# A layer norm plus masked attention kernel: the later groups' statistics taken from the transposed blocks again, the first two graphs interleaved by pieces, the second group's statistics made on ScalarE

## The chip, the cores and the metric

The kernel runs on one core of one Trainium2 chip. The time is the device time of one execution in microseconds. The kernel before has a median of 2884.72 us over three runs (2884.47 to 2885.43). Lower is better.

## The reference

128 graphs of 128 nodes with 768 features (`x`, float32), each with a 128 x 128 matrix of edge weights (`adj`). One layer is computed: a layer norm over the features without weights, a ReLU, three products with 768 x 768 weights, attention with 12 heads of 64 features that is masked and shifted by `adj`, and the sum with `x`.

```python
h = jnp.maximum(_layernorm(x, axis=-1), 0.0)
q, k, v = (split_heads(h @ W + b) for W, b in ((Wq, bq), (Wk, bk), (Wv, bv)))
scores = einsum('bhqd,bhkd->bhqk', q, k) / sqrt(64) + beta * adj[:, None]
scores = jnp.where(adj[:, None] > 0, scores, -9e15)
out = x + merge_heads(softmax(scores) @ v)
```

`_layernorm` is `(x - mean) / sqrt(var + 1e-5)`.

## The kernel before

The graphs are worked on in 32 groups of four (`GRP`); G counts the groups. A group goes through three slices of products on TensorE: `qk0` (queries and keys of heads 0 to 5), `v` (values) and `qk1` (queries and keys of heads 6 to 11). The normed, transposed activations of a group are taken as 2 x 3 blocks and each slice's weights as 3 x 3, and a slice is 15 products of sums of blocks (`PRODUCTS`, L66) in place of the 2 x 3 x 3 = 18 plain ones. A product is eight matrix multiplications (`product`, L355, all recorded at L371). The profile shows each as two passes, so a product is 16 passes. The products of a slice are added up in four PSUM banks, the chains a, b, c and d: when a product is done, its chain's bank is read by VectorE (L382, L387, L396) or ScalarE (L392), and only then may the chain's next product start. In the slice `qk0` of group 0 `plain_slice` (L520, products at L533) makes the 18 plain products.

The order of the work is written by hand: `todo[n]` holds what is issued after product n of a slice, and the loop over G (L647) fills it. The first part of group G's attention (`scores`, then three times `attend`) stands in its slices `v` and `qk1`, the second part in the slice `qk0` of group G+1. A scheduling layer then orders the instructions of each engine by when their inputs are expected, so that what has no gate moves ahead of its place. `tc.issue_after(i)` is such a gate: what is issued under it stays behind instruction i on its engine.

The lines that the change and the prediction touch:

- `load_x` (L151) loads a graph's x transposed by blocks of 32 x 32 (four loads of 96 KB), so that VectorE's 32 x 32 transposition (`to_hT`, L310, recorded at L315) makes the activations with features on the partitions. In this layout a row's features lie spread over four partitions. `stats` (L225) takes four statistics of 192 elements a graph; `moments_1` (L235, products at L241) and `moments_2` (L251, products at L255) add up the four partitions of a row with a small product with the matrix `mean8` each. Then follow the root on GpSimd (L262), the shift (L264) and the 16 norms on ScalarE (`norm`, L304, recorded at L308). Groups 1 and 2 go this way.
- Groups 3 to 31 instead take the statistics from a second copy of x in rows: `load_halves` (L271, two loads of 192 KB a graph), `row_stats` (L277, L283 and L284), `row_moments` (L286) with the root at L294, and 16 loads of 1 KB (L299) that spread the results over the partitions as `norm` wants them. `row_stats`, `norm` and `bias_1` of these groups are gated on the last addition of a product (`behind`, L653).
- `bias_1` (L332) and `bias_2` (L348) make the mask and shift of a group's scores out of `adj`; they use VectorE, a memset on GpSimd (L339) and a square on ScalarE (L346).
- Group 0's graphs 0 and 1 come in rows (L158). `rows_1` (L557) makes a graph's statistics and its root (L571), `rows_2` (L574) norms it in three pieces on VectorE (L579), transposes them on TensorE (L584) and applies the ReLU on ScalarE (L589). TensorE first runs 18 warm-up products (L595). Graph 0 is transposed as a whole and multiplied with the first column of weights, then `second` (L600) does the same for graph 1. Graphs 2 and 3 come in blocks.
- Group 1's x (L663) is loaded behind the weights of `qk1` (L674) on SyncE's queue; its statistics stand in slice `v` of G=0 (L695) on VectorE, beside the sums of weights (`sum_weights`, L197).

Of the kernel before, what the change touches and what calls it, by code (L numbers as in the profile page):

```python
# [10 lines left out]
F32 = mybir.dt.float32  # L11
# [6 lines left out]
P = 128  # L18
# [96 lines left out]
def direct(ctx, tc, x, adj, wq, bq, wk, bk, wv, bv, beta, out, bad):  # L115
# [115 lines left out]

    def halves(G, lo, hi, n):
        return st[G].rearrange("p b (h m) -> p b h m", h=2)[:, lo:hi, :, n]
# [34 lines left out]

    rows = {}

    def load_halves(G, g):  # L271

        for h in range(2):
            t = rows[G, g, h] = work.tile([P, VH], F32, tag=("adj", "adjT")[h], name=f"half_{G}_{g}_{h}", bufs=1)
            nc.sync.dma_start(t, x[G * GRP + g, :, h * VH:(h + 1) * VH])

    def row_stats(G, g):  # L277

        if g == 0:
            rows[G] = stat.tile([P, GRP, 2, nc.vector.BN_STATS_DIM], F32, tag="strow", name=f"strow_{G}", bufs=1)  # L280
            rows[G, "mv"] = stat.tile([P, GRP, nc.vector.BN_AGGR_DIM], F32, tag="mvrow", name=f"mvrow_{G}", bufs=1)
        for h in range(2):
            nc.vector.bn_stats(rows[G][:, g, h, :], rows[G, g, h])  # L283
        nc.vector.bn_aggr(rows[G, "mv"][:, g, :], rows[G][:, g])  # L284

    def row_moments(G):  # L286

        mv = rows[G, "mv"]
        ve = stat.tile([P, GRP], F32, tag="verow", name=f"verow_{G}", bufs=1)
        nc.vector.tensor_scalar(ve, mv[:, :, 1], EPS, None, op0=ALU.add)  # L290
        mean = stat.tile([P, GRP], F32, tag="meanrow", name=f"meanrow_{G}", bufs=1)
        nc.vector.tensor_scalar(mean, mv[:, :, 0], -1.0, None, op0=ALU.mult)
        t = stat.tile([P, 2, GRP], F32, tag="row2", name=f"row2_{G}", bufs=1)
        nc.gpsimd.tensor_tensor(t[:, 0], ve, nhalf.to_broadcast([P, GRP]), ALU.pow)  # L294
        nc.gpsimd.tensor_tensor(t[:, 1], mean, t[:, 0], ALU.mult)
        to = stat.tile([P, NB, 2, GRP], F32, tag="block2", name=f"block2_{G}", bufs=1)
        for b in range(NB):
            for a in range(NB):
                nc.sync.dma_start(to[a * SQ:(a + 1) * SQ, b], t[b * SQ:(b + 1) * SQ])  # L299
        for g in range(GRP):  # L300
            for b in range(NB):
                rstd[G, g * NB + b], shift[G, g * NB + b] = to[:, b, 0, g:g + 1], to[:, b, 1, g:g + 1]
# [217 lines left out]
    def plain_slice(G, sl, todo):  # L520

        n = 0
        for r in range(2):
            for j in range(3):
# [4 lines left out]
                for at, k in [(at, k) for at in parts for k in range(3)]:  # L529
                    a, b = A[G, f"A{r}{k}"], wt[sl, f"B{k}{j}"]  # L530
                    for i in range(2):
                        for c in range(2):
                            last = nc.tensor.matmul(p[:, i, at], b[:, c, i * P:(i + 1) * P], a[:, c, at],  # L533
                                                    start=(k == 0 and i == 0 and c == 0), stop=(c == 1),
                                                    skip_group_check=True)
                    if at is not parts[-1]:
                        if k == 2:
                            with tc.issue_after(last.ins):
                                second()
                        continue  # L540
                    if k == 2:
                        t = qk[G, sl, r, j] = work.tile([P, 2, H2], F32, tag="qk", name=f"{sl}_{G}_{r}_{j}", bufs=8)
                        oc = j + 3 * int(sl[2])
                        for i in range(2):
                            nc.scalar.activation(t[:, i, :], p[:, i, :], AF.Identity, bias=bqk[:, i, oc:oc + 1])
                        give(bank)
                    for f in todo.get(n, ()):
                        f()
# [329 lines left out]
```

## Time and profile before

| | us |
|---|---|
| median of three runs | 2884.72 |
| the profiled execution | 2884.47 |
| its span, from the first to the last instruction | 2882.7 |
| TensorE busy | 2872.4 |
| VectorE busy | 1955.9 |
| ScalarE busy | 806.5 |
| GpSimd busy | 316.9 |

The mean granted clock of TensorE is 0.999. A matrix multiplication of 128 x 256 is busy for 379 ns in the profile, but the passes overlap: one starts about every 0.108 us, so a product takes 1.727 us. A stage of TensorE (three slices, and the attention in between) takes 89.17 us.

The first stage, from the timeline:

| | start, us |
|---|---|
| warm-up products on TensorE | 2.15 |
| first graph's first statistics on VectorE | 4.79 |
| first piece of graph 0 (L579) | 8.24 |
| first transposition on TensorE (L584) | 8.90 |
| first plain product (L533) | 9.92 |
| graph 1's plain products | 13.46 |
| weights of `qk1`, first load issued | 27.70 |
| x of group 1, first load issued | 38.68 |
| slice `v` of G=0 | 43.10 |
| scores of G=0 (L417) | 73.35 |

How to read the profile's lines: a line of the timeline has the start and length in microseconds, the engine (PE is TensorE, PEld its weight loads, DVE VectorE, ACT ScalarE, POOL GpSimd, SP SyncE; a q behind the name means the engine's queue, which issues DMAs), the line of the kernel, the operation, the tile written and the tiles read, the shapes, the number of instructions merged, and in brackets how long the engine had been idle and what ended that. A line of the chain of waits has the start, the length and the group of instructions; the chain is followed back from the last instruction to what released each one.

### The profile page before, as it was taken

The page shows a single profiled execution, that of the slowest core. Times are in us where ns is not written, and L with a number is a line of the kernel's source. Part 1 is how long each engine was busy: PE and PEld are TensorE (multiplying, and loading weights), DVE is VectorE, ACT ScalarE, POOL GpSimd, SP SyncE. Part 2 cuts the span into 40 slices and gives each one's busy share as a digit, 9 for nine tenths or more (in the row PEclk, how much of TensorE's full clock was granted, in tenths as well). Part 3 has the DMA queues.
Part 4 walks back from the last instruction along what each step waited for, and adds up shares of the span by engine and source line. Part 5 has one row for each costly group of instructions (what it writes and reads, how often), then busy time and mean ns, then how long its engine had stood idle before and what let it go on. Part 6 is the DMA issues. An engine that isn't in the chain of part 4 may idle for free.

```text
span 2882.7 us, 81559 instructions
## 1 busy us (share of the span) xinstructions
PE 2872.4 (100%) x35330; PEld 2014.5 (70%) x35330; DVE 1955.9 (68%) x4511; ACT 806.5 (28%) x1750; POOL 316.9 (11%) x304
## 2 busy tenths in 40 slices
PE   9999999999999999999999999999999999999999
PEld 7666677666677676776667766677666677666776
DVE  7866666666666666666766666666666666666665
ACT  2422322232222323313232132322223222322221
POOL 1111111111011010110101101011101111110110
PEclk9999999999999999999999999999999999999999
DMA  6222233222232222322223322233222232222311
GB/s 167 77 62 76 58 84 87 73 71 67 75 88 80 64 74 68 87 86 63 76 65 86 90 60 82 60 85 88 69 75 62 80 88 75 69 70 72 88 41 39
DMA packets 413467, 218.31 MB, mean 76 GB/s; under 512 B 110384, under 2 KB 412720, under 8 KB 413104
## 3 DMA queue, kind: packets, MB, share of 16 engines
q1 hardware_dynamic: 411232, 212.66, 26.8%
q8 instruction: 277, 4.54, 0.6%
q10 hardware_dynamic: 1872, 0.40, 0.1%
q14 instruction: 86, 0.70, 0.1%
HBM read 162.14 MB, written 50.33 MB: 74 GB/s over the span
## 4 chain that ended last, share of the span: by engine, by line
PE 99%; DVE 1%; issue 0%; POOL 0%; POOLq 0%
PE bank L371 85%; PE bank L417 6%; PE bank L452 6%; PE bank L533 1%; PE bank L595 0%; DVE A L315 0%; DVE qk_T L206 0%; DVE qk L396 0%; DVE S L321 0%; DVE e L421 0%; PE bank L472 0%; PE bank L489 0%; PE bank L584 0%; DVE e L476 0%; DVE xo L497 0%
## 5 line engine op out<-in xcount | busy, mean ns | idle before, releaser
L371 PE MATMUL bank<-S,qk_T 128*64 128x256 f32 x7056 | 822.5, 379 | 0.8 <-ACT qk L392 0.8
L396 DVE TENSOR_TENSOR qk<-qk,bank 128x512 f32<-128x512 f32 x630 | 426.6, 677 | 411.8 <-PE bank L371 406.3
L371 PEld LDWEIGHTS bank<-S,qk_T 128*64 128x64 f32 x7056 | 503.8, 137 | 256.1 <-ACT e L424 5.2
L392 ACT ACTIVATE qk<-bank,bqk 128x256 f32<-128x256 f32 x756 | 315.8, 469 | 1149.3 <-PE bank L371 962.8
L457 POOL TENSOR_TENSOR xo<-xo,o 128x512 f32<-128x512 f32 x189 | 253.5, 1342 | 2075.2 <-DVE o L436 1777.9
L371 PE MATMUL bank<-S,qk_B 128*64 128x256 f32 x4032 | 478.2, 379 | 1.0 <-DVE qk L396 1.0
L371 PE MATMUL bank<-A,qk_T 128*64 128x256 f32 x4032 | 478.6, 379 | 0.4 <-DVE qk L396 0.4
L371 PE MATMUL bank<-v_T,S 128*64 128x256 f32 x3584 | 421.8, 380 | 0.0
L424 ACT ACTIVATE e<-e 128x512 f32<-128x512 f32 x378 | 227.8, 628 | 642.8 <-DVE e L421 641.8
L371 PEld LDWEIGHTS bank<-A,qk_T 128*64 128x64 f32 x4032 | 284.3, 137 | 137.0 <-DVE qk L396 0.5
L387 DVE TENSOR_TENSOR v<-v,bank 128x512 f32<-128x512 f32 x320 | 219.8, 687 | 232.6 <-PE bank L371 230.8
L371 PEld LDWEIGHTS bank<-S,qk_B 128*64 128x64 f32 x4032 | 278.6, 137 | 128.9 <-DVE qk L396 1.4
L371 PEld LDWEIGHTS bank<-v_T,S 128*64 128x64 f32 x3584 | 254.7, 137 | 130.4 <-issue 5.7
L421 DVE SCALAR_TENSOR_TENSOR e<-bank,biasT 128x512 f32<-128x512 f32 x378 | 231.7, 682 | 109.1 <-PE bank L417 109.1
L371 PE MATMUL bank<-v_B,S 128*64 128x256 f32 x2048 | 243.2, 379 | 0.0
L371 PE MATMUL bank<-v_T,A 128*64 128x256 f32 x2048 | 237.9, 379 | 0.0
L308 ACT ACTIVATE x<-x,block 128x192 f32<-128x192 f32 x464 | 217.3, 535 | 39.9 <-DMA block<-row 39.1
L452 PEld LDWEIGHTS bank<-v,e 128*64 128x64 f32 x6048 | 208.6, 138 | 27.3
L315 DVE STREAM_TRANSPOSE A<-x 128x256 f32<-128x256 f32 x378 | 211.8, 612 | 4.0 <-ACT x L308 4.0
L452 PE MATMUL bank<-v,e 128*64 128x65 f32 x6048 | 208.3, 221 | 0.0
L382 DVE TENSOR_TENSOR v<-bv_b,bank 128x512 f32<-128x512 f32 x192 | 131.8, 687 | 105.2 <-PE bank L371 105.2
L371 PEld LDWEIGHTS bank<-v_B,S 128*64 128x64 f32 x2048 | 147.1, 137 | 73.9
(90 smaller groups left out, 1603.6 us busy)
## 6 DMA issues: line engine op xcount, KB each, us to landing
x<-in_x_dram SPq DMA_DIRECT2D x504, 96.0 KB, 2.6
xo<-in_x_dram SPq DMA_DIRECT2D x189, 256.0 KB, 3.0
out_dram<-xo SPq DMA_DIRECT2D x189, 256.0 KB, 2.6
half<-in_x_dram SPq DMA_DIRECT2D x232, 192.0 KB, 2.8
adj<-in_adj_dram SPq DMA_DIRECT2D x128, 64.0 KB, 3.0
block<-row SPq DMA_DIRECT2D x464, 1.0 KB, 1.7
qk_T<-in_L_gnn_Wq_dram SPq DMA_DIRECT2D x10, 128.0 KB, 3.7
qk_T<-in_L_gnn_Wk_dram SPq DMA_DIRECT2D x10, 128.0 KB, 3.8
```

The costliest lines, as they stand in the source:

```text
L308: nc.scalar.activation(t, t, AF.Relu, bias=shift[G, n], scale=rstd[G, n])
L315: last = nc.vector.transpose(t[:, :, g * N:(g + 1) * N].rearrange("p c (b i) -> p c b i", i=SQ), src)
L371: nc.tensor.matmul(p[q:q + HD, i, :], lhs[:, q:q + HD], rhs, start=(first and i == 0 and c == 0), stop=(c == 1), skip_group_check=True)
L382: added[G] = nc.vector.tensor_tensor(o4, bias[:, None, :, :].to_broadcast([P, 2, 4, HD]), p.rearrange("p g (h d) -> p g h d", d=HD), ALU.a ...
L387: added[G] = nc.vector.tensor_tensor(o, o, got, ALU.add if sign > 0 else ALU.subtract)
L392: nc.scalar.activation(t[:, i, :], p[:, i, :], AF.Identity, bias=bqk[:, i, oc:oc + 1], scale=float(sign))
L396: added[G] = nc.vector.tensor_tensor(t, t, p, ALU.add if sign > 0 else ALU.subtract)
L417: nc.tensor.matmul(ps[oc, i][k:k + HD, g * N:(g + 1) * N], t[r, 1, at][:, k:k + HD], t[r, 0, at], start=True, stop=True)
L421: taken[0] = nc.vector.scalar_tensor_tensor(e, ps[oc, i].rearrange("p (g n) -> p g n", g=GRP), SCORE_CAP * ISCALE, biasT[G], op0=ALU.min, ...
L424: nc.scalar.activation(e, e, AF.Exp, scale=1.0 / ISCALE)
L452: nc.tensor.matmul(pa[q:q + HD, 2 * g + i, :], es[G, oc, i][:, 2 * r + g, q:q + HD], vt[G, "v", r, h // 4][:, 4 * g + h % 4, :], start=Tru ...
L457: nc.gpsimd.tensor_add(t, t, o.rearrange("p a (b j) d -> p (a b) (j d)", j=2))
```

## The change

1. `load_halves`, `row_stats` and `row_moments` go. Every group after the first has its statistics from the blocks (`stats`, `moments_1`, `moments_2`), and the gates `behind` go too. For groups 3 and later `stats` has no gate.
2. `stats_by_act` is new. It makes the statistics of group 1 on ScalarE: one pass with an accumulated sum for the mean of each block, one with an accumulated sum of squares for the deviations. It is called for graphs 0 and 1 at place 8 of `qk0` and for graphs 2 and 3 at place 0 of `v` of G=0. The norms of group 1 are placed one product sooner.
3. The loads of group 1's x for graphs 0 and 1 are issued ahead of the weights of `qk1` on SyncE's queue.
4. Graphs 0 and 1 of group 0 are interleaved: VectorE's operations stand in one line (`begin`), graph 1's statistics between graph 0's pieces, and TensorE's transpositions stand between the plain products (`PIECES`, `transposed`).

```diff
+    def stats_by_act(G, lo, hi):
+        if G not in st:
+            st[G] = stat.tile([P, GRP * NB, nc.vector.BN_STATS_DIM], F32, tag="st", name=f"st_{G}", bufs=2)
+        m = stat.tile([P, hi - lo], F32, tag=f"mean{lo}", name=f"mean_{G}_{lo}", bufs=1)
+        for step in range(2):
+            for n in range(lo, hi):
+                junk = work.tile([P, QD], F32, tag="e", name=f"junk_{G}_{step}_{n}", bufs=6)
+                t = xg[G, n // NB][:, n % NB, :]
+                if step:
+                    nc.scalar.activation(junk, t, AF.Square, bias=m[:, n - lo:n - lo + 1], scale=math.sqrt(0.5),
+                                         accum_out=st[G][:, n, 2:3])
+                else:
+                    nc.scalar.activation(junk, t, AF.Copy, scale=1.0 / QD, accum_out=st[G][:, n, 1:2])
+            if not step:
+                nc.scalar.activation(m, st[G][:, lo:hi, 1], AF.Copy, scale=-math.sqrt(0.5))
+        nc.scalar.copy(st[G][:, lo:hi, 4:6], st[G][:, lo:hi, 1:3])
...
-    def load_halves(G, g):
...
-    def row_stats(G, g):
...
-    def row_moments(G):
...
@@ plain_slice
-                for at, k in [(at, k) for at in parts for k in range(3)]:
...
-                    if at is not parts[-1]:
-                        if k == 2:
-                            with tc.issue_after(last.ins):
-                                second()
-                        continue
...
+                for g, at in enumerate(parts):
+                    for k in range(3):
+                        if len(parts) == 2:
+                            for piece in PIECES[g, k]:
+                                transposed(*piece)
+                        a, b = A[G, f"A{r}{k}"], wt[sl, f"B{k}{j}"]
                         for i in range(2):
+                            for c in range(2):
+                                line("pe", nc.tensor.matmul, p[:, i, at], b[:, c, i * P:(i + 1) * P], a[:, c, at],
+                                     start=(k == 0 and i == 0 and c == 0), stop=(c == 1), skip_group_check=True)
...
+    PIECES = {(0, 0): ((0, 0), (0, 1)), (0, 1): ((0, 2),), (0, 2): (), (1, 0): ((1, 0), (1, 1)), (1, 1): ((1, 2),),
+              (1, 2): ()}
...
+    def transposed(g, k):
+        bank = take()
+        p = bank[:, 0:H2].rearrange("p (c i) -> p c i", c=2)
+        for c in range(2):
+            line("pe", nc.tensor.transpose, p[:, c, :], rows[g, k][:, c, :], ident)
...
+        nc.scalar.activation(A[0, name][:, :, g * N:(g + 1) * N], p, AF.Relu)
+        give(bank)
...
+        stats_of(0, 0)
+        stats_of(0, 1)
+        root(0)
+        stats_of(1, 0)
+        piece(0, 0)
+        stats_of(1, 1)
+        piece(0, 1)
+        root(1)
+        piece(0, 2)
         for k in range(3):
+            piece(1, k)
...
@@ the loop over G
         if G + 1 < NG:
             for g in range(GRP):
-                then(6, lambda g=g: load_x(G + 1, g, (nc.sync,)))
+                if G:
+                    then(6, lambda g=g: load_x(G + 1, g, (nc.sync,)))
                 if G == 1:
                     then(11 + g, lambda g=g: behind_scores(stats, G + 1, g))
                 elif G:
-                    then((0, 5, 8, 11)[g], lambda g=g: load_halves(G + 1, g))
-                    then((4, 7, 10, 13)[g], lambda g=g: behind(row_stats, G + 1, g))
-            if G > 1:
-                raw = []
-                then(14, lambda: raw.append(load_adj(G + 1)))
-                then(14, lambda: row_moments(G + 1))
+                    then(11 + g, lambda g=g: stats(G + 1, g))
         if not G:
+            for g in range(2):
+                load_x(1, g, (nc.sync,))
             load_weights("qk1", AS_SUMMED)
+            for g in range(2, GRP):
+                then(6, lambda g=g: load_x(1, g, (nc.sync,)))
+            then(8, lambda: stats_by_act(1, 0, 2 * NB))
...
             at = 3 if G else 5
+            if not G:
+                then(0, lambda: stats_by_act(1, 2 * NB, 4 * NB))
             for g in range(GRP):
-                if not G:
-                    then(g, lambda g=g: stats(G + 1, g))
-                then(at + 5 + g, lambda g=g: behind(norm, G + 1, g) if G > 1 else norm(G + 1, g))
-            if G < 2:
-                then(at, lambda: got.extend(moments_1(G + 1, 0, GRP * NB)))
-                then(at + (3 if G else 2), lambda: moments_2(G + 1, 0, GRP * NB, *got[:2]))
+                then(at + (5 if G else 4) + g, lambda g=g: norm(G + 1, g))
+            then(at, lambda: got.extend(moments_1(G + 1, 0, GRP * NB)))
+            then(at + (3 if G else 2), lambda: moments_2(G + 1, 0, GRP * NB, *got[:2]))
             if G:
-                then(8, lambda: got.append(behind(bias_1, G + 1, raw.pop()) if raw else bias_1(G + 1, load_adj(G + 1))))
-                then(12, lambda: bias_2(G + 1, got[-1]))
+                then(8, lambda: got.append(bias_1(G + 1, load_adj(G + 1))))
+                then(12, lambda: bias_2(G + 1, got[2]))
```

In the changed kernel the lines have other numbers: the small products of `moments_1` and `moments_2` are at L260 and L274, the products at L355, the bank reads at L376 (ScalarE), L366, L371 and L380 (VectorE), the scores' products at L401, the norms at L292 and the passes of `stats_by_act` at L243 and L246.

## The prediction

> **What bounds the kernel now.** I read the chain of waits first, by engine. TensorE carries it from end to end:
>
> ```profile
> PE 99%; DVE 1%; issue 0%; POOL 0%; POOLq 0%
> ```
>
> So a part is worth what it adds to TensorE's own stream, or what makes TensorE wait. Then I read the same chain between 130 and 330 us, where one stage still has the statistics products (L241, L255) and the next no longer has:
>
> ```profile
> 142.13 3.60 PE bank L371 x32
> 145.74 0.09 PE bank L241 x4
> 145.83 5.21 PE bank L371 x48
> 151.03 0.09 PE bank L255 x4
> 151.12 24.20 PE bank L371 x224
> ...
> 231.53 32.96 PE bank L371 x304
> ```
>
> Columns: start, length, what. Stage G=1 makes group 2's statistics the old way: its five pieces run from 142.13 to 175.32, 33.19 us for 304 product passes and 8 small ones. Stage G=2 needs 32.96 us for the same 304. The small products therefore cost 0.23 us a group (their own 0.18 and 0.05 more around them), and nothing waits at them. The stages after G=2 repeat every 89.17 us (231.53, 320.70, 409.87) without a wait on TensorE.
>
> Third, the timeline of stage G=0, the only one in which TensorE waits between its first product and the last stage (0.77, 0.40 and 0.99 us):
>
> ```profile
> 64.44 0.31 PE L255 MATMUL bank<-dev,mean 128*64 128x32 f32 x4
> 65.63 2.91 POOL L262 TENSOR_TENSOR rstd<-ve,nhalf 128x16 f32<-128x16 f32 x1 [42.66 <-DVE ve L260]
> 68.62 0.42 POOL L264 TENSOR_TENSOR shift<-mean,rstd 128x16 f32<-128x16 f32 x1
> 69.07 7.12 ACT L308 ACTIVATE x<-x,shift,rstd 128x192 f32<-128x192 f32 x16 [25.03 <-POOL shift L264]
> 76.10 1.53 ACT L392 ACTIVATE qk<-bank,bqk 128x256 f32<-128x256 f32 x4
> 76.96 3.67 PE L371 MATMUL bank<-S,qk_T 128*64 128x256 f32 x32 [0.77 <-ACT qk L392]
> 97.65 1.95 PE L371 MATMUL bank<-A,qk_T 128*64 128x256 f32 x16 [0.40 <-DVE qk L396]
> 100.59 1.95 PE L371 MATMUL bank<-S,qk_B 128*64 128x256 f32 x16 [0.99 <-DVE qk L396]
> ```
>
> The reader should see a chain: statistics products, a root on GpSimd, 16 norms on ScalarE, and behind them in ScalarE's order the reads of two banks (L392) that TensorE needs before the third product of slice qk1.
>
> **Step 1, later groups.** Row statistics go for groups 3 to 31, 29 groups. Gone per group: 8 loads of 192 KB and 16 of 1 KB on SyncE's queue, 8 statistics of 384 elements and 4 aggregates on VectorE. None is on the chain: nothing to gain. Back come 16 statistics of 192 elements, four small VectorE operations twice, and 8 passes on TensorE: 29 x 0.23 = +6.7 us. On GpSimd the root takes 2.91 instead of 1.02 us; in G=1 the same root and norms are done about 162.7 (151.91 + 0.17, then 2.91, 0.42 and 16 x 0.445), before the transposes at 165.62, and no other GpSimd work is queued there.
>
> **Step 2, where these statistics stand.** They lose their gate. In the changed program's order they stand in slice qk1, one stage ahead, between VectorE's additions, and the sooner ones can wait for x. The trace has no such row, so I bound it. VectorE's rows there, and the queue's:
>
> ```profile
> 270.65 0.69 DVE L396 TENSOR_TENSOR qk<-qk,bank 128x512 f32<-128x512 f32 x1 [0.97 <-PE bank L371]
> 278.18 0.68 DVE L396 TENSOR_TENSOR qk<-qk,bank 128x512 f32<-128x512 f32 x1
> ...
> 287.36 3.68 DVE L421 SCALAR_TENSOR_TENSOR e<-bank,biasT 128x512 f32<-128x512 f32 x6 [3.19 <-PE bank L417]
> ```
>
> ```profile
> 270.48 0.99 SPq L155 DMA_DIRECT2D x<-in_x_dram x2
> 281.92 1.50 SPq L155 DMA_DIRECT2D x<-in_x_dram x3
> ```
>
> Four statistics take 1.13 us (timeline, L230). The group's 16 are 4.5 us; VectorE idles 5.7 us between 264.6 and 287.4. Graph 1's x lands about 273.9 (270.97 + the 3.0 us of that window), so VectorE, free at 272.97, waits 0.9 us for it. Adding the moved operations in order, the addition at 278.18 ends about 279.85 instead of 278.86. The product that needs its bank starts at 280.94: 1.1 us are left. Graph 3's x waits for a store, which waits for GpSimd behind VectorE: last load issued near 285, landed 287.3, its statistics end at 288.4 and the score reads start 1.05 us late. Behind them the next addition waits for a GpSimd memset (0.52) and a ScalarE square (0.63) too, since the bias of the group after next loses its gate as well; it ends about 295.5, and its bank is needed at 298.78. Price 0; lower bound 0, since TensorE has no wait to lose there; upper bound 0.5 us a group (x 1.6 us later), 14.5 us.
>
> **Step 3, statistics of group 1 on ScalarE.** Sixteen VectorE statistics (4.5 us) leave slice v of G=0, where VectorE is busy 27.06 of 31 us and TensorE never waits: gain 0. ScalarE gets 32 passes. The nearest row is the norm, 16 in 7.12 us, 0.445 each. Half of the first pass runs while ScalarE waits for qk0's banks; 24 passes are left after 43.2, so 43.2 + 24 x 0.445 + some 1.6 for four small operations and a bank read = 55.5. No row has an accumulated output; at twice the norm's price they end at 66.2.
>
> But the changed program's order has the first small products in the thirteenth product of slice v (before: the eleventh) and the second ones behind the first pass of the fifteenth (before: the thirteenth). TensorE runs in order, so readiness at 55.5 brings nothing. With 1.727 us a product, the second small products come at 67.95 instead of 64.44. VectorE then has an addition and a weight sum in front of the last small operation: it starts at 69.7, not 65.39, 4.3 us later. GpSimd's 2.91 and 0.42 follow, the norms run from 73.35 to 80.4, and the bank reads let TensorE go on at 81.25 instead of 76.96.
>
> What is late next: VectorE. It still has transposes of group 1 to do, whose x is normalised in time, so of the 4.3 us it idles about 2.3 at the next two additions. TensorE meets VectorE's additions later, and its waits of 0.40 and 0.99 us vanish. The product at 100.59 then starts at about 103.05: **+2.45 us**. Bounds: 0 (if VectorE alone decided up to 100.6) and +4.3.
>
> That wait, from 76.2 to 81.25, would be the longest of the run; so far none inside is over 0.99 us, and the granted clock is 1.00 until the end. Only there, among waits of 0.60, 0.27 and 0.96 us, does it fall (columns: stretch, length, busy time and count of PE, PEld, DVE, ACT, POOL, then clock, DMA share, GB/s):
>
> ```profile
> 2873.00:2878.00 5.00, 3.50 (x82) 2.65 (x80) 4.63 (x18) 1.55 (x4) 0.00 (x0) 1.00 0.34 102
> 2878.00:2883.00 5.00, 0.23 (x2) 0.09 (x2) 1.08 (x5) 0.00 (x0) 0.00 (x0) 0.53 0.21 61
> ```
>
> What a fall would cost I bound by the start's warm-up: 36 passes in 6.91 us against 24 of the same shape in 2.68 later, 2.9 us lost. I take 0 of 0 to 2.9, since no row shows a fall inside the stream.
>
> The Trainium skill speaks against this step (TensorE: Matmul & The Clock Gate, section "What's actually happening"): the array falls to half clock after an idle window of some 3.4 us, which runs free of the kernel, and needs about as long a busy one to rise. A wait of 5 us holds a whole such window about every second time; then an estimated 3.4 us would run at half speed, 1.7 us lost, and the sum would be 2895.7 instead of 2894.0.
>
> **Step 4, x of group 1 sooner.** Eight loads at 0.53 us on SyncE's queue go ahead of qk1's 18 weight loads: their first issue moves from 27.70 to about 32, their first use on VectorE is at 45.70, landing takes up to 5.4: hidden by 8 us. The other eight x loads keep their place (last issue 47.2).
>
> **Step 5, the first two graphs.** Piece (0,0) comes 0.85 us sooner (7.39 for 8.24), but the warm-up products hold TensorE until 9.06. The first product can start at 9.8 instead of 10.09; graph 1's pieces come 0.5 us later (its root is behind a memset, and starts at 9.25), and TensorE idles 0.3 before graph 1's first product, with one transposition (0.22) now after it. Ends at 16.35 against 16.14: **+0.2**; bounds -0.3 (the sooner start alone) and +0.5 (the idle time and the transposition alone).
>
> **Sum.** 2884.47 (profiled execution: span 2882.7 and 1.8 around it) + 6.7 + 2.45 + 0.2 = 2893.8; the median of the runs is 0.25 above the profiled one: **2894.0**.
>
> **Rivals.**
> - VectorE becomes the bound in slice qk1 of every later stage. For it: 4.5 us of statistics into 5.7 us of idle time, and waits for x in between. Against: 1.1 us to spare. It decides from x landing after 275. At 0.4 us a group 11.6 more: 2905.6.
> - ScalarE's passes are late. Decides above 0.83 us a pass, when 43.2 + 1.6 + 24 passes pass 64.95. At 1.0 us: 68.8, so 3.9 us more: 2897.9. For it: no row of an accumulated output; against: the norm's 0.445.
> - On the other side: the first stage gets shorter. Its place is 76 to 100.6 us: if TensorE need not wait for ScalarE there (norms done by 76.1, which decides) and VectorE, relieved, runs ahead, the three waits go, 2.2 us; with 6.7 for the later groups 2889.2, no difference that a measurement can tell. For it: VectorE's long stretch in the chain, 74.55 to 100.55; against: the order above.
> - The small products are hidden in the stream (0 for 0.23): 2887.3. Against: the two stages compared above.
>
> **How the numbers follow.** Sum 0.61; VectorE bound 0.15; ScalarE late 0.09; first stage shorter 0.09; small products free or anything else 0.06. A difference of 0.2% (5.8 us) is about what a measurement of this kernel tells from none. The first three are slower, less 0.01 for a small sum: 0.84; the last two lie within 0.2% but for 0.03 left for faster: 0.13. Range 2889 to 2903: down to the shorter first stage, up to 0.3 us a group in step 2, or a fallen clock and late passes together.
>
> **What would show it.** Stages of 89.40 us, with L260 and L274 of 0.09 us each; the 16 norms of G=0 starting near 73.3, TensorE's wait for the bank reads about 5 us, no VectorE waits near 100; in slice qk1 of later stages no TensorE wait, and a VectorE wait for x of about 1 us. Wrong, if stages take over 89.6, or TensorE goes on before 80 in G=0.

## The result, and the profile after

| | before | after |
|---|---|---|
| median, us | 2884.99 (six runs, 2884.47 to 2885.43) | 2897.60 (six runs, 2896.82 to 2898.66) |
| ratio, 95% interval | 1 | 1.0044 [1.0031, 1.0057] |
| profiled execution, span | 2884.47, 2882.7 | 2896.82, 2895.0 |
| TensorE busy | 2872.4 | 2881.1 |
| VectorE, ScalarE, GpSimd busy | 1955.9, 806.5, 316.9 | 1958.0, 816.0, 370.8 |

The changed kernel is 12.6 us slower. In the profiled executions it is 12.3, and these split into the start with stage G=0 (5.22: the last product of this stage that waits for VectorE starts at 105.81, before at 100.59) and the 29 stages after it (7.12). The tail is the same.

The chain of waits of the changed kernel, by engine, still runs through TensorE:

```profile
PE 98%; DVE 1%; ACT 0%; DMA 0%; issue 0%; POOL 0%; SPq 0%; DVEq 0%; POOLq 0%
```

The same chain between 130 and 330 us (start, length, what):

```profile
147.35 3.60 PE bank L355 x32
150.96 0.09 PE bank L260 x4
151.04 5.21 PE bank L355 x48
156.25 0.09 PE bank L274 x4
156.34 24.20 PE bank L355 x224
...
236.75 3.60 PE bank L355 x32
240.35 0.09 PE bank L260 x4
240.44 5.21 PE bank L355 x48
245.65 0.09 PE bank L274 x4
245.74 24.20 PE bank L355 x224
```

Stage G=2 now has the same five pieces as G=1: the small products L260 and L274 stand in it, and the next stage comes after 89.40 us (156.34 to 245.74) for 89.17. All later stages take 89.40, but for one of 89.66 and one of 89.50. Nothing waits at the small products.

The timeline of stage G=0 (the first line is the end of ScalarE's statistics of group 1, the second the first small products):

```profile
56.22 0.21 ACT L249 COPY st<-st 128x16 f32<-128x16 f32 x1
...
64.88 0.30 PE L260 MATMUL bank<-st,mean 128*64 128x32 f32 x2
...
67.99 0.30 PE L274 MATMUL bank<-dev,mean 128*64 128x32 f32 x4
69.99 2.91 POOL L281 TENSOR_TENSOR rstd<-ve,nhalf 128x16 f32<-128x16 f32 x1 [46.89 <-DVE ve L279]
72.98 0.22 POOL L283 TENSOR_TENSOR shift<-mean,rstd 128x16 f32<-128x16 f32 x1
73.23 7.12 ACT L292 ACTIVATE x<-x,shift,rstd 128x192 f32<-128x192 f32 x16 [4.71 <-POOL shift L283]
80.26 1.53 ACT L376 ACTIVATE qk<-bank,bqk 128x256 f32<-128x256 f32 x4
81.12 5.94 PE L355 MATMUL bank<-S,qk_T 128*64 128x256 f32 x32 [4.84 <-ACT qk L376]
105.81 1.95 PE L355 MATMUL bank<-S,qk_B 128*64 128x256 f32 x16 [0.41 <-DVE qk L380]
```

The reader should see the chain of before, moved by 3.6 to 4.4 us: small products, root, 16 norms, bank reads, and TensorE behind them. The wait is 4.84 us where it was 0.77. And the 32 passes after it last 5.94 us where they lasted 3.67. The windows of the same stretch say why (columns as in the prediction):

```profile
76.00:81.00 5.00, 0.28 (x12) 0.04 (x4) 5.00 (x10) 5.00 (x13) 0.00 (x0) 0.79 0.01 3
81.00:86.00 5.00, 4.88 (x24) 2.80 (x26) 1.54 (x3) 4.69 (x11) 0.00 (x0) 0.53 0.00 0
86.00:91.00 5.00, 5.00 (x66) 3.46 (x64) 3.82 (x7) 1.28 (x4) 0.00 (x0) 1.00 0.22 61
```

The granted clock fell to a half during the wait and stayed there until 85.7: TensorE was busy for nearly all of 81 to 86 us, yet only 24 passes are recorded in it, where 4.88 us at the usual 0.108 us a pass would hold 45.

Last, the place of the moved statistics (L230) in a later stage, in the timeline between 262 and 300 us:

```profile
274.23 1.14 DVE L230 BATCH_NORM_STATS2 st<-x 128x6 f32<-128x192 f32 x4
...
279.04 0.36 DVE L230 BATCH_NORM_STATS2 st<-x 128x6 f32<-128x192 f32 x1 [0.62 <-DMA x<-in_x_dram]
...
293.51 1.26 DVE L230 BATCH_NORM_STATS2 st<-x 128x6 f32<-128x192 f32 x4 [2.90 <-DMA x<-in_x_dram]
...
294.45 3.67 PE L355 MATMUL bank<-S,qk_T 128*64 128x256 f32 x32
294.69 3.66 DVE L405 SCALAR_TENSOR_TENSOR e<-bank,biasT 128x512 f32<-128x512 f32 x6
```

VectorE does wait for x, in all 75.9 us in this kernel, and the last four statistics make its score reads (L405) start late. But the TensorE row between them has no bracket: it waits for none of that.

The longest stage (89.66) is different, in the timeline between 538 and 563 us:

```profile
548.89 0.36 DVE L230 BATCH_NORM_STATS2 st<-x 128x6 f32<-128x192 f32 x1 [2.26 <-DMA x<-in_x_dram]
...
554.06 0.68 DVE L380 TENSOR_TENSOR qk<-qk,bank 128x512 f32<-128x512 f32 x1
...
554.80 3.22 PEld L355 LDWEIGHTS bank<-S,qk_T 128*64 128x64 f32 x32 [0.49 <-DVE qk L380]
```

Here x came later, VectorE waited 2.26 us for it in front of its additions, and TensorE's weight loads then waited for one of these. The stage of 89.50 has the same two waits, of 2.08 and 0.34 us.

### The profile page after: what moved, and what is told of

It reads as the page before. It is cut to its first block, busy times and chain, and to the rows that moved or that the text cites. A ratio compares the mean times of both kernels' runs of the same rounds, so it can differ in the third digit from the quotient of the medians.

```text
span 2895.0 us, 81404 instructions
## 1 busy us (share of the span) xinstructions
PE 2881.1 (100%) x35562; PEld 2022.2 (70%) x35562; DVE 1958.0 (68%) x4727; ACT 816.0 (28%) x1818; POOL 370.8 (13%) x304
## 4 chain that ended last, share of the span: by engine, by line
PE 98%; DVE 1%; ACT 0%; DMA 0%; issue 0%; POOL 0%; SPq 0%; DVEq 0%; POOLq 0%
PE bank L355 85%; PE bank L436 6%; PE bank L401 6%; PE bank L547 1%; ACT x L292 0%; DVE qk_T L206 0%; DVE S L305 0%; DMA x<-in_x_dram 0%; DVE qk L380 0%; DMA bqk<-in_L_gnn_bk_dram 0%; PE bank L260 0%; POOL rstd L281 0%; PE bank L274 0%; DVE A L299 0%; PE bank L456 0%
## 5 line engine op out<-in xcount | busy, mean ns | idle before, releaser
L355 PE MATMUL bank<-S,qk_T 128*64 128x256 f32 x7056 | 824.8, 380 | 4.9 <-ACT qk L376 4.8
L355 PEld LDWEIGHTS bank<-S,qk_T 128*64 128x64 f32 x7056 | 504.7, 137 | 261.9 <-issue 6.0
L380 DVE TENSOR_TENSOR qk<-qk,bank 128x512 f32<-128x512 f32 x630 | 428.7, 681 | 343.6 <-PE bank L355 340.7
L376 ACT ACTIVATE qk<-bank,bqk 128x256 f32<-128x256 f32 x756 | 312.3, 472 | 1010.0 <-PE bank L355 811.2
L355 PE MATMUL bank<-S,qk_B 128*64 128x256 f32 x4032 | 478.2, 379 | 0.4 <-DVE qk L380 0.4
L355 PE MATMUL bank<-A,qk_T 128*64 128x256 f32 x4032 | 478.5, 379 | 0.0
L355 PE MATMUL bank<-v_T,S 128*64 128x256 f32 x3584 | 422.5, 380 | 0.0
L371 DVE TENSOR_TENSOR v<-v,bank 128x512 f32<-128x512 f32 x320 | 220.1, 688 | 298.9 <-PE bank L355 298.9
L355 PEld LDWEIGHTS bank<-A,qk_T 128*64 128x64 f32 x4032 | 284.3, 137 | 136.4 <-issue 0.2
L355 PEld LDWEIGHTS bank<-S,qk_B 128*64 128x64 f32 x4032 | 278.6, 137 | 128.3 <-DVE qk L380 0.9
L355 PEld LDWEIGHTS bank<-v_T,S 128*64 128x64 f32 x3584 | 252.0, 137 | 126.1 <-issue 5.7
L292 ACT ACTIVATE x<-x,shift,rstd 128x192 f32<-128x192 f32 x504 | 224.3, 533 | 329.6 <-POOL shift L283 329.6
L355 PE MATMUL bank<-v_B,S 128*64 128x256 f32 x2048 | 243.7, 380 | 0.0
L405 DVE SCALAR_TENSOR_TENSOR e<-bank,biasT 128x512 f32<-128x512 f32 x378 | 231.2, 680 | 16.7 <-PE bank L401 16.7
L355 PE MATMUL bank<-v_T,A 128*64 128x256 f32 x2048 | 237.5, 379 | 0.0
L366 DVE TENSOR_TENSOR v<-bv_b,bank 128x512 f32<-128x512 f32 x192 | 131.8, 687 | 112.7 <-PE bank L355 112.7
L230 DVE BATCH_NORM_STATS2 st<-x 128x6 f32<-128x192 f32 x488 | 149.9, 344 | 76.2 <-DMA x<-in_x_dram 75.9
```

The source lines that it names most:

```text
L230: nc.vector.bn_stats(st[G][:, g * NB + b, :], xg[G, g][:, b, :])
L292: nc.scalar.activation(t, t, AF.Relu, bias=shift[G, n], scale=rstd[G, n])
L355: nc.tensor.matmul(p[q:q + HD, i, :], lhs[:, q:q + HD], rhs, start=(first and i == 0 and c == 0), stop=(c == 1), skip_group_check=True)
L371: added[G] = nc.vector.tensor_tensor(o, o, got, ALU.add if sign > 0 else ALU.subtract)
L380: added[G] = nc.vector.tensor_tensor(t, t, p, ALU.add if sign > 0 else ALU.subtract)
L405: taken[0] = nc.vector.scalar_tensor_tensor(e, ps[oc, i].rearrange("p (g n) -> p g n", g=GRP), SCORE_CAP * ISCALE, biasT[G], op0=ALU.min, ...
```

## The experiments

All times are medians, and those of the kernel before on the same chips are 2884.98 to 2885.18. The start differs from execution to execution: the last 104 passes of slice qk0 begin between 20.08 and 21.17 us in the kernels with the new start and between 20.29 and 20.60 in those with the old one. To compare stage G=0 without that, I also read from the chains the time from the first of these passes (L533 before, L547 after) to group 2's second small products in G=1 (L255 before, L274 after):

| kernel | first stage by these marks, us | against before | later stages, us | median, us |
|---|---|---|---|---|
| before | 130.52 | | 89.17 | 2884.99 |
| after | 135.58 | +5.06 | 89.40 | 2897.60 |
| e1_rows_late | 135.00 | +4.48 | 89.17 | 2889.95 |
| e2_vector_stats | 131.68 | +1.16 | 89.40 | 2893.00 |
| e3_old_start | 135.04 | +4.52 | 89.40 | 2896.66 |
| e4_filler | 133.67 | +3.15 | 89.40 | 2894.90 |
| e5_early | 132.35 | +1.83 | 89.40 | 2894.48 |
| e6_doubled | 134.99 | +4.47 | 89.68 | 2904.55 |
| e7_gated | 135.63 | +5.11 | 89.40 | 2896.62 |
| e8_best | 131.77 | +1.25 | 89.17 | 2886.63 |
| e9_all | 131.36 | +0.84 | 89.17 | 2885.14 |
| e10_old | 131.40 | +0.88 | 89.17 | 2885.43 |
| e11_first | 132.05 | +1.53 | 89.40 | 2893.31 |
| e12_bias | 129.18 | -1.34 | 89.17 | 2883.61 |

**e1_rows_late: the later groups' row statistics back.**

```diff
-                    then(11 + g, lambda g=g: stats(G + 1, g))
+                    then((0, 5, 8, 11)[g], lambda g=g: load_halves(G + 1, g))
+                    then((4, 7, 10, 13)[g], lambda g=g: behind(row_stats, G + 1, g))
+            if G > 1:
+                raw = []
+                then(14, lambda: raw.append(load_adj(G + 1)))
+                then(14, lambda: row_moments(G + 1))
...
```

> The changed kernel with part 1 undone: groups 3 to 31 take row statistics from a second load again; the rest of the change stays. My theory (the later stages lost their 0.23 us each to eight small product passes on TensorE): stages of 89.17 us from G=2 on, about 7 us less than the changed kernel, 2890.5 us, ratio to the kernel before 1.0019. Rival (the small products are hidden, and the whole difference lies in the first stage): 2897.6 us, ratio 1.0044. Rival (the second load itself cost something): below 2889 us.

Measured: 2889.95 us (2888.86 to 2891.44), ratio 1.0017 [1.0008, 1.0026], 7.65 less than the changed kernel. The stages are 89.17 again. So part 1 is worth the 7.1 us that the stages show. The other half microsecond is in stage G=0, which is as in the changed kernel but for its clock; more on that under e4.

**e6_doubled: the small products issued twice.** This tells TensorE's passes from the other work that came with them (VectorE's statistics, the order).

```diff
-        for q in range(0, P, HD):
+        for q in [q for q in range(0, P, HD) for n in range(1 + (G > 2))]:
```

> The changed kernel with each of the small statistics products of groups 3 to 31 issued twice (8 more passes in each of 29 stages; the results are the same). My theory (these passes are the whole price of the later stages): 29 x 0.2 to 0.23 = 5.8 to 6.7 us more than the changed kernel, 2903.4 to 2904.3 us, stages of 89.6. Rival (VectorE's statistics or the changed order cost, the passes are free): 2897.6 us.

Measured: 2904.55 us (2903.98 to 2906.76), 6.95 more than the changed kernel. The chain of this kernel between 236 and 340 us:

```profile
235.68 3.60 PE bank L355 x32
239.28 0.26 PE bank L260 x8
239.54 5.18 PE bank L355 x48
244.72 0.23 PE bank L274 x5
244.95 24.20 PE bank L355 x224
```

Eight more passes took L260 from 0.09 to 0.26 and L274 from 0.09 to 0.23, and the piece behind the first 0.03 less; the stage is 89.68, 0.28 more. (The chain shows five of the eight passes of L274; the timeline has all eight.) In 29 stages that is 8.1 us; the profiled executions differ by 7.2, since stage G=0 (0.6 us) and the start (0.5 us) are shorter here. So passes of 32 columns on this stream have a price of 0.03 us each, and they alone explain the usual later stage.

**e7_gated: the statistics back behind the score reads.**

```diff
-                if G == 1:
+                if G:
                     then(11 + g, lambda g=g: behind_scores(stats, G + 1, g))
-                elif G:
-                    then(11 + g, lambda g=g: stats(G + 1, g))
```

> The changed kernel with the statistics of groups 3 to 31 held behind the score reads on VectorE, as those of group 2 are, so that they stand in slice qk0 and no more between the additions of slice qk1. My theory (where they stand costs nothing, since TensorE waits for nothing there): 2897.6 us, within 0.5 of the changed kernel. Rival (statistics that wait for x hold up VectorE's additions): 1 us or more less than the changed kernel.

Measured: 2896.62 us (2895.80 to 2897.24), 1.0 less than the changed kernel: between the two expectations. The profiled executions differ by 0.2 only (spans 2894.8 and 2895.0), and the stages are 89.40 in both; what this kernel does not have in its profile are the two longer stages of the changed one (0.26 and 0.10). So where the statistics stand costs nothing in a usual stage. It does make the rare longer one: in all seven profiled kernels whose later statistics have no gate (the changed one, e2, e3, e4, e5, e6 and e11) TensorE's weight loads wait for an addition of VectorE in two to six of the later stages, 0.15 to 0.80 us each time, and in e7_gated and the kernels with row statistics in none. In the profiled executions that is 0.36 us; that it is the whole 1.0 between the medians is not shown, and the ranges of the two overlap.

**e2_vector_stats: group 1's statistics on VectorE, its x loaded and its norms placed as before.**

```diff
-            for g in range(2):
-                load_x(1, g, (nc.sync,))
             load_weights("qk1", AS_SUMMED)
-            for g in range(2, GRP):
+            for g in range(GRP):
                 then(6, lambda g=g: load_x(1, g, (nc.sync,)))
-            then(8, lambda: stats_by_act(1, 0, 2 * NB))
...
-            if not G:
-                then(0, lambda: stats_by_act(1, 2 * NB, 4 * NB))
             for g in range(GRP):
-                then(at + (5 if G else 4) + g, lambda g=g: norm(G + 1, g))
+                if not G:
+                    then(g, lambda g=g: stats(1, g))
+                then(at + 5 + g, lambda g=g: norm(G + 1, g))
```

> The changed kernel with group 1's statistics made by VectorE again, its x loaded as before. My theory (stage G=0 lost about 5 us to the wait for the bank reads behind the 16 norms and the clock that fell behind it): the norms start near 69 us, TensorE waits 0.7 to 1 us for them, the granted clock stays 1.00, about 5 us less than the changed kernel, 2892.5 us, ratio 1.0026. Rival (the late small products stay late whoever makes the statistics): 2897 us or more.

Measured: 2893.00 us (2892.48 to 2894.55), 4.6 less than the changed kernel. Its timeline:

```profile
64.26 0.31 PE L274 MATMUL bank<-dev,mean 128*64 128x32 f32 x4 [0.30 <-DVE dev L267]
...
68.91 7.12 ACT L292 ACTIVATE x<-x,shift,rstd 128x192 f32<-128x192 f32 x16 [25.25 <-POOL shift L283]
...
76.80 3.67 PE L355 MATMUL bank<-S,qk_T 128*64 128x256 f32 x32 [0.36 <-ACT qk L376]
```

The small products are sooner by 3.7 us than in the changed kernel, the norms start at 68.91 for 73.23, the wait is 0.36 us and the 32 passes last 3.67: the loss of stage G=0 belongs to the statistics on ScalarE or to the sooner loads of x, which this run takes back together; e5_early, which keeps both and has not the long wait, shows that it is the place of the small products. Most of the 1.16 us that remain against the kernel before are VectorE's: TensorE waits 2.3 us for its additions (1.39 before), and the 0.30 at the small products are new.

**e4_filler: TensorE kept busy in its wait.** Forty passes into a bank that nobody reads, behind the scores at 75.6 us.

```diff
+    def fill():
+        bank = take()
+        with tc.issue_after(taken["pe"].ins):
+            for n in range(20):
+                nc.tensor.matmul(bank[:, 0:P], ident, ident, start=True, stop=True)
+        give(bank)
...
+            todo[SC_AT].insert(1, fill)
```

> The changed kernel with 40 extra passes of 128x128 on TensorE in its wait of stage G=0 (behind the scores at 74 to 75 us), which write to a bank that nobody reads; nothing else moves. My theory (the fall of the granted clock costs about 2.5 us of the 5.2 that this stage lost): the clock stays 1.00 between 78 and 86 us, the first 32 passes after the wait take 3.6 us for 5.94, and the kernel takes 2895.1 us, 2.5 us less than the changed one. Rival (the clock is not the cost, the wait alone is): 2897.6 us or more. Rival (the extra passes push the third product later): over 2898 us.

Measured: 2894.90 us (2894.64 to 2897.22), 2.7 less than the changed kernel, with 4.73 us more of work. Four of its five runs are below all runs of the changed kernel; the fifth, 2897.22, is not. Its timeline and windows:

```profile
72.64 7.12 ACT L292 ACTIVATE x<-x,shift,rstd 128x192 f32<-128x192 f32 x16 [4.71 <-POOL shift L283]
...
75.62 4.73 PE L664 MATMUL bank<-ident 128*128 128x128 f32 x40
79.67 1.53 ACT L376 ACTIVATE qk<-bank,bqk 128x256 f32<-128x256 f32 x4
80.53 3.67 PE L355 MATMUL bank<-S,qk_T 128*64 128x256 f32 x32 [0.18 <-ACT qk L376]
```

```profile
76.00:81.00 5.00, 4.82 (x44) 4.51 (x44) 5.00 (x10) 5.00 (x13) 0.00 (x0) 1.00 0.00 0
81.00:86.00 5.00, 5.00 (x50) 3.32 (x48) 5.00 (x10) 4.04 (x9) 0.00 (x0) 1.00 0.34 97
```

The norms take their 7.12 us and TensorE's useful work goes on behind them as before; only the clock is different, 1.00 throughout, and the 32 passes are back at 3.67 us. So the fallen clock is a cost of its own, beside the wait: 5.94 - 3.67 = 2.27 us in the changed kernel's profiled execution. By the marks the stage is 1.91 us shorter, since TensorE, sooner at VectorE's additions, waits 0.3 us longer for them.

In e1_rows_late the wait is the same 4.84 us (75.82 to 80.66), but the windows show the fall later and shorter:

```profile
80.66 5.36 PE L390 MATMUL bank<-S,qk_T 128*64 128x256 f32 x32 [4.84 <-ACT qk L411]
```

```profile
80.00:81.00 1.00, 0.34 (x4) 0.27 (x6) 1.00 (x3) 1.00 (x4) 0.00 (x0) 0.99 0.00 0
81.00:82.00 1.00, 1.00 (x8) 0.60 (x6) 1.00 (x2) 1.00 (x3) 0.00 (x0) 0.50 0.00 0
82.00:83.00 1.00, 1.00 (x7) 0.49 (x4) 0.09 (x1) 1.00 (x3) 0.00 (x0) 0.50 0.00 0
83.00:84.00 1.00, 1.00 (x8) 0.63 (x6) 0.00 (x0) 1.00 (x3) 0.00 (x0) 0.50 0.00 0
84.00:85.00 1.00, 1.00 (x12) 0.60 (x10) 0.00 (x0) 1.00 (x3) 0.00 (x0) 0.80 0.00 0
```

The clock falls only when TensorE has already gone on. Adding up twice what each stretch lacks to 1.00 (0.02 + 3 + 0.40) gives 3.42 us at half speed, and 5.36 us for the 32 passes: 1.7 lost. That is the 0.6 us by which this stage G=0 is shorter than the changed kernel's.

**e3_old_start: the first two graphs one after the other.** `rows_1`, `rows_2`, `second` and the products of `plain_slice` are those of the kernel before; the rest is the changed kernel.

```diff
-                for g, at in enumerate(parts):
-                    for k in range(3):
-                        if len(parts) == 2:
-                            for piece in PIECES[g, k]:
-                                transposed(*piece)
...
+                for at, k in [(at, k) for at in parts for k in range(3)]:
...
-    begin()
+    got = [rows_1(g) for g in range(2)]
+    rows_2(0, *got[0])
```

> The changed kernel with the old start of the first two graphs (one after the other). My theory (the new start costs 0.16 us): 2897.4 us, 0 to 0.4 us less than the changed kernel, which is within the error. Rival (the sooner first product brought time that something later hides): 1 us or more slower than the changed kernel.

Measured: 2896.66 us (2896.06 to 2897.81), 0.9 less than the changed kernel, in ranges that overlap, and with the shorter fall of the clock (5.36 us for the 32 passes) that is worth 0.6 by itself in the profiled execution. The rival (1 us or more slower) is out; that the new start costs the 0.16 us of the first theory is not shown.

**e5_early: group 1's small products where they are ready.** The first go before the ninth product of slice v in stage G=0, the second three passes behind, and what follows on TensorE is gated on them.

```diff
-            product(G, sl, n, order)
+            with ExitStack() as behind:
+                for step, first_at in ((1, 8), (2, 11)):
+                    if G == 0 and (sl == "qk1" or sl == "v" and at >= first_at):
+                        behind.enter_context(tc.issue_after(pm[1, 0, step].ins))
+                product(G, sl, n, order)
...
-            todo.setdefault(SC_AT, []).insert(0, lambda: scores(0, 0))
+            todo.setdefault(SC_AT, []).insert(0, lambda: behind_moments(scores, 0, 0))
```

> The changed kernel with group 1's small products held in their place on TensorE: the first before the ninth product of slice v of G=0, the second three passes of the ninth later; what TensorE does after them waits for them. My theory (the statistics of ScalarE are ready at 56.4 us, and only the place of the small products behind later work makes the norms start at 73): the norms start near 62, the wait of about 5 us at 76 is gone, the clock stays 1.00, TensorE pays about 1 us for waiting at the second small products; 2892.5 us, 5 us less than the changed kernel. Rival (VectorE's work at 64 to 74 us decides, and the norms stay late): 2896 us or more.

Measured: 2894.48 us (2893.98 to 2895.30), 3.1 less than the changed kernel, not 5. The small products are at 57.48 and 59.90 us, the norms at 63.97, the clock stays 1.00 and the wait of 4.84 us is gone, as expected. But the list of waits between 40 and 110 us shows what took its place:

```profile
PE bank L355 <- DVE qk L380: 2.3, 2, 1.3
PE bank L274 <- DVE dev L267: 1.3, 1, 1.3
PE bank L355 <- ACT qk L376: 0.2, 1, 0.2
```

TensorE pays 1.3 us at the second small products, which VectorE prepares, and 2.3 at two of VectorE's additions near 100 us, where the changed kernel waits 0.41 once. Without the long wait, TensorE runs into VectorE's stream, which does not pause from 76 us on.

**e8_best and e9_all: both costs removed.** e8_best is e1_rows_late and e5_early together (the "run before but two" of its expectation is e5_early). e9_all adds two shifts in stage G=0 (lines against e8_best):

```diff
-                for step, first_at in ((1, 8), (2, 11)):
+                for step, first_at in ((1, 8), (2, 9)):
...
-            then(at + (3 if G else 2), lambda: moments_2(G + 1, 0, GRP * NB, *got[:2]))
+            then(at + 3, lambda: behind_pe(moments_2, G + 1, 0, GRP * NB, *got[:2]))
...
-            with tc.issue_after(added[G].ins if G else taken[0].ins):
+            with tc.issue_after(added[G].ins if G else pm[1, 0, 2].ins if n in ("A01", "A02") else taken[0].ins):
...
-                then(at if G else max(at, SC_AT), lambda n=n: transposes(n))
+                then(at if G or n in ("A01", "A02") else max(at, SC_AT), lambda n=n: transposes(n))
```

> Row statistics for groups 3 to 31 (part 1 undone) and group 1's small products held early as in the run before but two: both costs removed, ScalarE's statistics, the sooner x and the interleaved start kept. My theory (the two costs are separate and add up: 7.6 and about 5 us): 2885 us, ratio 1.0000, 12.6 us less than the changed kernel. Rival (the second load of the rows and the early products collide in the first stages): over 2888 us.

> As e8 (row statistics for groups 3 to 31, early small products), with two more shifts in stage G=0: the second small products come after the whole ninth product of slice v, 1.7 us later, and two of group 1's six transposes on VectorE (A01, A02) no longer stand behind the score reads, so that they fall into VectorE's idle time before these. My theory (e8's 1.6 us over the kernel before are TensorE's 1.3 us at the second small products and 2.3 us at two additions of VectorE, less what the kernel before waits itself): both waits go, 3 us less than e8, 2883.5 us, ratio 0.9995. Rival (VectorE's additions are late for another reason): 2886 us.

Measured: e8_best 2886.63 us (ratio 1.0006 [0.9997, 1.0015]), e9_all 2885.14 (0.9999 [0.9990, 1.0008]). The two costs are separate and add up: 7.65 and 3.12 us by e1_rows_late and e5_early, 10.97 for both together in e8_best. The expected 2885 counted 5 us for the second. Of the 3 us that e9_all was to bring it brought 1.5: the wait at the second small products fell from 1.3 to 0.4, but the first of VectorE's early transposes now waits 3.13 us for the norms in front of an addition of slice v, for which TensorE then waits 0.6, and the two waits near 100 us are still 2.0.

**e10_old and e11_first.** e10_old is e9_all with the start of the kernel before; e11_first is the changed kernel with e9_all's shifts in stage G=0 and its own later stages.

> As e9 with the old start of the first two graphs. My theory (the new start costs 0.2 us in TensorE's stream): 2883.3 us, within 0.5 of e9. Rival (the interleaved start is worth something once the first stage has no wait): 1 us or more slower than e9.

> The changed kernel with the two shifts and the early small products of e9 in stage G=0, and its later stages as they are. My theory (statistics on ScalarE cost nothing if the small products stand where they are ready): the whole loss of G=0 is gone, 2890.5 us, 7 us less than the changed kernel and as much over e9 as the small products of 29 groups cost (6.7 to 7.6). Rival: 2892.5 us or more.

Measured: e10_old 2885.43 us, 0.3 from e9_all, in ranges that overlap: the interleaved start is not shown to be worth anything here either. e11_first 2893.31 (2891.24 to 2894.19), 4.3 less than the changed kernel and not 7; it has the same waits near 100 us as e9_all, one of 1.0 for an addition of slice v (0.6 in e9_all), and one of 0.6 for ScalarE's statistics at the first small products. Against e9_all it is 8.2 us longer, of which 0.7 by the marks above (132.05 for 131.36) is in stage G=0; the rest is the later stages' 6.7 and their longer ones.

**e12_bias: VectorE's stream in stage G=0 cleared.** The lines are against e9_all.

```diff
-            then(9, lambda: behind_scores(bias_2, 0, early[0]))
-            then(13, lambda: early.append(behind_scores(bias_1, 1, load_adj(1))))
+            then(13, lambda: behind_adds(bias_2, 0, early[0]))
+            then(14, lambda: early.append(behind_adds(bias_1, 1, load_adj(1))))
...
-            for n, at in enumerate(SUMS_AT):
-                then(at, lambda n=n: sum_acts(G + 1, n))
+            for n, at in enumerate(SUMS_AT if G else (5, 11, 6, 6, 7, 8, 12, 13, 14, 14, 14)):
+                then(at, lambda n=n, at=at: behind_adds(sum_acts, 1, n) if at > 10 and not G else sum_acts(G + 1, n))
```

> As e9, with more of VectorE's work moved behind the last additions of stage G=0: the maximum of group 0's bias, the whole bias of group 1, and five of the sums of group 1's activations. My theory (VectorE works without a pause from 76 to 102 us, and TensorE's two waits of 1.25 and 0.79 us for its additions are the work standing in front of them): the waits at 98.8 and 101.5 shrink to under 0.5 us together, 2883.6 us, ratio 0.9995, 1.5 us less than e9. Rival (the moved work is late in the next stage): TensorE waits there, 2885 us or more.

Measured: 2883.61 us (2882.59 to 2884.99), ratio 0.9995 [0.9985, 1.0004]. All of TensorE's waits for others after 20 us, in this kernel:

```profile
PE bank L814 <- DVE over L812: 1.0, 1, 1.0
PE bank L508 <- ACT e L498: 0.9, 2, 0.6
PE bank L390 <- DVE v L406: 0.6, 1, 0.6
PE bank L274 <- DVE dev L267: 0.4, 1, 0.4
```

The first two are in the tail. The waits near 100 us are gone and none came in the next stage, so it was the work in front of VectorE's additions. By the marks stage G=0 is 1.34 us shorter than in the kernel before. The median is 1.6 us below that of the kernel before (2885.18 on the same chip), but the interval holds 1: faster than the changed kernel by 14 us, and not shown to be faster than the one before it.

## Why the prediction was right, and where it was short

The forecast (slower, 2894.0, range 2889 to 2903) holds the measured 2897.60; the sum was 3.6 us low.

- **Step 1, +6.7 for the later groups: right.** Of the 7.12 in the trace 29 x 0.23 = 6.7 are its, 0.36 lie in the two longer stages (step 2), and the rest is rounding. e1_rows_late takes it back, and e6_doubled shows it to be TensorE's small products.
- **Step 2, price 0: right in a usual stage, too low in a few.** The waits for x came as foreseen, and later in the stage than estimated (2.90 us before the last four statistics), and TensorE has no wait there. In two of the 29 stages x came so late that the 1.1 us to spare did not do, and TensorE waited for VectorE: 0.36 us in all, inside the bounds of 0 and 14.5. The rival in which VectorE becomes the bound in every later stage is out.
- **Step 3, the chain: right, its price somewhat low.** Norms 73.23 to 80.35 (73.35 to 80.4 foreseen), TensorE on at 81.12 (81.25), ScalarE's statistics done at 56.43 (55.5), so that they waited for their small products and the rival "passes late" is out: e5_early consumes them 7.4 us sooner, at 57.48. The waits for VectorE's additions fell from 1.39 to 0.41 us and did not vanish. Of the first stage's 5.06 us, the passes at half clock took 2.27, and the other 2.79 answer to the predicted 2.45; without the fall, in e4_filler, the stage is 3.15 longer than before. The prediction does not show how it came from 4.3 and 2.3 to 2.45, so that it came this close may in part be luck.
- **Step 3, the fall of the clock: the term that failed.** "I take 0 of 0 to 2.9, since no row shows a fall inside the stream" was wrong, though the bounds held: the same text foresaw a wait of 5 us, five times the longest in that stream, and no row there could speak for so long a wait. It measured 2.27 us in the profiled execution, and e4_filler, which keeps TensorE busy through the same wait, is 2.7 us faster by its median and 1.9 by the marks. This is the largest part of the 3.6 us missing; the rest is 0.4 in step 2, 0.3 in step 3, and 0.5 by which the median lies further above the profiled execution than it did before.
- **Step 4, hidden: nothing speaks against it.** It was not tried alone.
- **Step 5, +0.2: not shown.** In the profiled execution the first product came sooner (9.54 for 9.92), graph 1's last piece later, and the stage's last 104 passes start 0.16 us later. But this mark lies anywhere from 20.08 to 21.17 us in the profiles with the new start, and e3_old_start and e10_old, 0.9 faster and 0.3 slower than their partners, show no price either way.
- The rival on the other side, a shorter first stage, did not happen in the change as it stands; e12_bias shows what it would have asked for: small products in a place where they are ready, and VectorE's work cleared from in front of its additions.

The Trainium skill (TensorE: Matmul & The Clock Gate, section "What's actually happening") says that the clock follows a window of about 3.4 us that runs free of the kernel. In length these runs agree: the half-speed stretches are 3.42 us in e1_rows_late and, by the same sum over stretches of 1 us, 6.8 us in the changed kernel, once and twice that window, at different places after the same wait. They do not agree with a fall only after a whole idle window, on which the prediction's "about every second time" rests: in the changed kernel the clock falls at 78.9 us (0.79 over the 5 us to 81.00 leaves 2.1 us at half speed), 2.6 us after TensorE's wait began at 76.28, and all five profiled executions with a wait of 4.7 to 4.8 us and nothing in it (the changed kernel, e1, e3, e6 and e7) show a fall. The prediction's estimate by this section, 1.7 us lost and 2895.7 in all, was nearer than its 0: in e1, e3 and e6 the 32 passes lose 1.7.

## What to carry to other kernels

When an engine that runs in order bounds a kernel, work moved to an idle engine helps only as soon as the bounding engine's own order lets its result through: here the statistics were ready at 56.4 us and their small products stood at 65 and 68. Price a new wait of several microseconds on TensorE twice, once for the wait and once for the half clock behind it; passes that nobody reads, put into the wait (40 here), buy the second part back. And when one wait is removed, look at once for the stream that stands behind it: here VectorE's additions, which took back 2 of 5 us until they too were cleared.

## What the runs showed of the hardware

- The clock's fall after a wait of 4.7 to 4.8 us differs between executions: half speed for 3.42 us, beginning after TensorE had gone on, or for 6.8 us, beginning 2.6 to 2.8 us into the wait. The 32 passes behind it took 5.36 us in the first case and 5.94 or 6.00 in the second, for 3.67. Waits of 1.3 us and less were followed by no fall inside the stream.
- A pass with an accumulated output on ScalarE is two records. Of these 128 x 192 squares the pass was 0.44 us and the reading of the accumulator 0.19, of which half lay under the end of the pass and half under the start of the next: one started every 0.44 us (0.35 for the plain copies), no slower than the norms of the same shape (0.445).
- Products of 128 x 32 cost 0.03 us a pass in a full stream of TensorE, though the profile shows four of them as busy for 0.26 us.
